# Last part of a two-layer graph kernel: residual rows reloaded by pairs, first results accumulated on a ScalarE copy of bank 1, softmaxes and tails in a new order

## The chip, the cores and the metric

The kernel runs on one core of one Trainium2 chip. A core has five engines that run their own instruction queues side by side: TensorE (PE in the profile, its weight loads PEld), VectorE (DVE), ScalarE (ACT), GpSimd (POOL) and SyncE (SP), which here only issues DMAs. An engine takes its instructions strictly in their order; an instruction that waits for a semaphore holds up all behind it. SBUF is the working memory, PSUM holds what TensorE writes, in eight banks of 128 x 512 fp32. [...]

The metric is device time in microseconds, as the median of runs. One further execution was taken by the hardware profiler; its instructions and waits are what the profile and the trace show. Times in the trace count from the start of its span.

## The reference, cut to what matters

```python
# x: (128, 128, 512), adj: (128, 128)     b = item, n = node, d = feature
# layer 0
A = einsum('od,bdn->bon', adj, x); C = A + b0[None, :, None]
x1 = layernorm(x + max over m of relu(A[..., None, :] + (C - A)[..., :, None]))
# layer 1: attention with 8 heads of 64, masked by adj
q, k, v = split(x1 @ w_qkv)
attn = softmax(where(adj == 0, -inf, q @ k.T * 64 ** -0.5))
o = (attn @ v) @ w_proj + b_proj
out = layernorm(x1 + o + layernorm(o) * ln_gamma + ln_beta)
```

All is fp32. Each of the 128 items is a 128 x 512 matrix, so an item fits one SBUF tile with nodes on the partitions.

## The kernel before, in words

Items are handled in pairs (64) and in groups of four (32). A loop of 61 rounds, one pair each, overlaps the stages of several pairs: layer 0 of a pair to come, scores and softmax of the present one, attention of the one before, projection and final normalizations ("tails") of older ones. Behind the loop stands the *last part*, written out by hand (from line 929 on), where the pipeline runs empty: the softmaxes of the last six items, the last v unit, two o units, the direct projections of the last four items, and the tails of the last sixteen. `L` is 127, the last item, so `L - 3` is the item 124; pairs are numbered 0 to 63, and `B // 2 - 8` is pair 56. All calls go through `pin`, which keeps the order in which they are written as the order of every engine's queue.

**Units.** The products with w_qkv and w_proj are computed for a group at once with seven half-size products in place of eight (class `Unit`, line 165). Product 1 goes into PSUM bank 1, and 6 and 7 are added to it; the partial sums after 1, 6 and 7 are copied out by ScalarE (`snap(1)` to `snap(3)`, line 185). Bank 2 takes product 2, bank 3 products 5 and later 3, bank 4 product 4. VectorE adds a bank and a snap to give one quarter of the output (`result`, line 190): (0,0) is bank 2 + snap 1, (1,1) bank 3 + snap 3, (1,0) bank 4 + snap 3, (0,1) bank 3 + snap 2 once product 3 has been added. The operands of products 3, 5, 6 and 7 are sums that GpSimd makes (`run_sums(o_sums(...))`, tile `s_o`). In the last part the output bias is put into banks 2, 3 and 4 of an o unit by ScalarE ahead of the products (`seed`, line 520). One unit's banks must have been read before the next unit may write them. The profile calls the banks `b_qk`, `b_v` and `b_o`.

**Softmax of an item.** `scores` (TensorE, eight matmuls into two banks), `softmax_max` (VectorE: scale and mask twice, then the maximum, tile `nmax`), `softmax_exp` (ScalarE: eight exponentials with row sums), `softmax_div` (VectorE), `prob_transpose` (VectorE, tile `pu`), `prob_write` and `prob_read` (SP: out to DRAM as `hop`, back in four pieces as `pT`, which finishes the transposition), `attend` (TensorE, bank `po` or `pa`) and `attend_copy` (ScalarE, to `oT`).

**Tail of an item.** Statistics of `o` (`bn`, two VectorE instructions; `finish_stats`, line 252: GpSimd adds epsilon, raises to the power -0.5 into `rs`, negates the mean and multiplies to `sh`), normalization of `o` on ScalarE (`tail_inner`), times gamma, plus `o`, plus the residual row on GpSimd (`tail_residual`, three instructions), statistics of that sum, normalization on ScalarE (`tail_outer`) and the store. The residual x1 + beta lies in DRAM as `spill`, written earlier by pairs; it is reloaded into `xr`, a tile with two buffers of one pair (`tail_reload`, line 555), or, for the last ten items, into the room that the query/key weights leave in SBUF, behind the reloaded w_proj (`last_load`, line 514, tile `wlast`; `tail_reload_one`, line 561, one item each). The last four items' tails go a shorter way: `fused_open` on VectorE makes (o - mean) * gamma and o + residual from `o`, `fused_close` joins both with `rs`. For two items ScalarE itself makes the statistics (`scalar_stats`, line 648), finished on GpSimd.

The lines that the change moves past one another are those of one hand-written list; the queue of SP follows it as the other engines' queues do. So a store that waits for a normalization holds up the reloads and `hop` transfers written behind it.

Of the kernel before, what the change touches and what calls it, by code (L numbers as in the profile page):

```python
# [16 lines left out]
def kernel(  # L17
# [145 lines left out]
    class Unit:  # L163
# [25 lines left out]

        def result(self, half, col):  # L190
            bank, k = {(0, 0): (2, 1), (0, 1): (3, 2), (1, 0): (4, 3), (1, 1): (3, 3)}[half, col]
            pin(
                nc.vector.tensor_tensor(  # L193
                    self.out[half, col], self.banks[bank], self.snaps[k], ALU.add
                )
            )
# [55 lines left out]
    def finish_stats(mv, keys, eng=None, fused=0):  # L252

        n = len(keys)
        if n == 0:
            return
        sh = small.tile([P, NC], F32, tag="sh", name=f"sh_{mv.name}")
        if eng is None:
            pin(nc.vector.tensor_scalar(sh[:, :n], mv[:, :n, 0], -1.0, None, ALU.mult))
# [3 lines left out]
        if eng is None:  # L263
            tt(nc.gpsimd, sh[:, :n], sh[:, :n], rs[:, :n], ALU.mult)
        elif n > fused:

            part = slice(fused, n)
            pin(eng.tensor_scalar(sh[:, part], mv[:, part, 0], -1.0, None, ALU.mult))
            tt(eng, sh[:, part], sh[:, part], rs[:, part], ALU.mult)
# [249 lines left out]

    def seed(unit, bank):  # L520
        cols = slice(HE, D) if bank == 3 else slice(0, HE)
        bias = bp_bc[:, cols].unsqueeze(1).to_broadcast([P, 2, HE])
# [38 lines left out]
    def tail_reload_one(b, place):  # L561
        rs_[b] = place
        pin(nc.sync.dma_start(out=place, in_=spill[b // 2][:, b % 2]))
# [71 lines left out]
    def stats(name, *items, eng=None, fused=0):  # L635

        mv = small.tile([P, NC, 2], F32, tag="mv", name=f"mv_{name}")
        for k, (kind, b) in enumerate(items):
            bn({"o": o_of, "z": zs.get, "y": xs.get}[kind](b), mv, k)
        finish_stats(mv, items, eng, fused)  # L640
        return mv
# [129 lines left out]
    for p in range(LAST + 1):  # L771
# [146 lines left out]
        if p == 1:  # L918
            weight_sums(wp, 0, HE)
        if f is not None:  # L920
# [8 lines left out]
    L = B - 1  # L929
    po_pa = ("po", "pa")  # L930
    pool = nc.gpsimd
# [8 lines left out]
    seed(o_u, 2)  # L940
# [3 lines left out]
    tail_inner(B // 2 - 7)  # L944
    softmax_max(L - 5)
    before.result(1, 0)
    softmax_max(L - 4)
    o_u.product(1)
    o_u.snap(1)
    o_u.product(2)  # L950
    softmax_exp(L - 5)
    seed(o_u, 4)
    o_u.result(0, 0)
    before.product(3)
    before.result(0, 1)
    tail_residual(B // 2 - 7)
    softmax_exp(L - 4, range(4))
    o_u.product(6)
    scores(L - 3)
    scores(L - 2, po_pa)  # L960
    o_u.snap(2)
    seed(o_u, 3)
    softmax_exp(L - 4, range(4, H))
    softmax_div(L - 5)
    prob_move(L - 5)
    o_u.product(4)
# [3 lines left out]
    softmax_exp(L - 3, range(4))  # L970
    o_u.snap(3)
    softmax_exp(L - 3, range(4, H))
    softmax_div(L - 4)
    prob_move(L - 4)
    softmax_max(L - 2)
    o_u.result(1, 1)
    o_u.result(1, 0)
    tail_outer(B // 2 - 8)
    tail_store(B // 2 - 8)
    tail_reload(B // 2 - 6)  # L980
    wlast, room = last_load()
    for t in range(L - 9, L + 1):
        tail_reload_one(t, room[:, t - L + 9])
    v_u.product(2)
    v_u.product(1)
    v_u.snap(1)
    stats("last_1", ("o", L - 9), ("o", L - 8), eng=pool)
    softmax_exp(L - 2, range(4))
    o_u.product(3)
    o_u.result(0, 1)  # L990
    v_u.result(0, 0)
    v_u.product(6)
    v_u.snap(2)
    softmax_exp(L - 2, range(4, H))
    for t in (L - 9, L - 8):
        tail_inner_one(t)
    tail_residual_one(L - 9)
    v_u.product(5)
    v_u.product(7)
    stats("last_2", ("o", L - 11), ("o", L - 10), eng=pool)  # L1000
    tail_residual_one(L - 8, [0])
# [3 lines left out]
    v_u.snap(3)  # L1005
    v_u.product(4)
    v_u.result(1, 1)
# [12 lines left out]
    scores(L, po_pa)  # L1020
    run_sums(o_sums(NG - 2))
    o_u = o_unit(NG - 2)
    seed(o_u, 2)
    for t in (L - 11, L - 10):
        tail_inner_one(t)
    softmax_max(L - 1)
    v_u.result(1, 0)
    v_u.product(3)
    softmax_max(L)
    softmax_exp(L - 1, range(4))  # L1030
    o_u.product(1)
    o_u.snap(1)
# [144 lines left out]
```

## Time and profile before

| | us |
|---|---|
| median of 3 runs | 1966.01 (1965.82 to 1967.39) |
| the profiled execution | 1967.67 |
| its span, first to last instruction | 1965.7 |
| around the span | 1.97 |

| stretch (us from the start) | length | TensorE busy | VectorE | ScalarE | GpSimd |
|---|---|---|---|---|---|
| 1868 to 1890 | 22.00 | 22.00 | 14.23 | 12.84 | 8.41 |
| 1890 to 1908 | 18.00 | 16.97 | 14.27 | 12.09 | 3.92 |
| 1908 to 1926 | 18.00 | 15.71 | 15.75 | 12.87 | 16.36 |
| 1926 to 1947 | 21.00 | 18.09 | 16.49 | 11.99 | 18.68 |
| 1947 to 1966 | 19.00 | 0.29 | 10.00 | 4.64 | 12.63 |

A row of a timeline gives the start, the duration, the engine, the line, the operation, the tiles written and read, the count, and in brackets how long the engine had been idle just before and what ended that. The loop fills the first 1870 us; the last part begins there. Times before and after are compared by medians of runs; sums over instructions are made against the profiled execution.

### The profile page before, as it was taken

What the parts mean: (1) busy time and instruction counts of PE and PEld (TensorE: products, weight loads), DVE (VectorE), ACT (ScalarE), POOL (GpSimd) and SP (SyncE); (2) the same over time, 40 slices, a digit from 0 to 9 for tenths busy, and PEclk for the clock granted to TensorE, in tenths of its full rate; (3) what the DMA queues carried; (4) which work ended last, traced back from release to release, by engine and by line L of the source; (5) the groups of instructions that cost most, each with busy time, mean ns of one, the idle gap of its engine ahead of it and who ended that gap; (6) DMA issues with size and microseconds to landing.
All of it is one profiled execution on the core that took longest, in us unless ns stands there. A gap on an engine that the chain in (4) does not pass through costs nothing.

```text
span 1965.7 us, 33048 instructions
## 1 busy us (share of the span) xinstructions
PE 1936.3 (99%) x11543; PEld 1639.7 (83%) x11543; DVE 1560.8 (79%) x2512; ACT 1062.2 (54%) x3084; POOL 1296.1 (66%) x824
## 2 busy tenths in 40 slices
PE   9999999999999999999999999999999999999995
PEld 6888888888888888888888888888888888888883
DVE  6767878778778788787787787887887877877876
ACT  3444655555545546555555455465565555554565
POOL 6336666767667677667676676676676766676748
PEclk9999999999999999999999999999999999999998
DMA  6747576576576676675765755766757667667554
GB/s 216 164 131 182 145 188 173 161 204 162 166 198 160 174 193 159 185 180 161 196 169 164 203 155 169 197 159 180 190 156 191 168 168 201 160 167 199 135 186 141
DMA packets 445654, 341.75 MB, mean 174 GB/s; under 512 B 276912, under 2 KB 378416, under 8 KB 445488
## 3 DMA queue, kind: packets, MB, share of 16 engines
q1 hardware_dynamic: 445056, 338.85, 64.2%
q8 instruction: 92, 1.51, 0.3%
q10 hardware_dynamic: 432, 0.79, 0.1%
q14 instruction: 74, 0.61, 0.1%
HBM read 172.82 MB, written 166.72 MB: 173 GB/s over the span
## 4 chain that ended last, share of the span: by engine, by line
PE 95%; DVE 2%; POOL 1%; DMA 1%; ACT 0%; issue 0%; SPq 0%; POOLq 0%; ACTq 0%; DVEq 0%
PE b_qk L74 39%; PE b_v L74 19%; PE b_o L74 18%; PE pss L74 6%; PE po L74 6%; PE pa L74 6%; POOL zl L77 1%; DMA x<-in_x_dram 0%; DMA wlast<-spill 0%; DVE s L77 0%; POOL rs_mv_last L77 0%; PE idle L74 0%; DVE pu L442 0%; DMA out_dram<-xr 0%; DVE s L402 0%
## 5 line engine op out<-in xcount | busy, mean ns | idle before, releaser
L74 PE MATMUL b_qk<-s_x,wqk 128*128 128x256 f32 x2048 | 473.3, 379 | 1.0 <-DVE s_x L77 0.7
L74 PEld LDWEIGHTS b_qk<-s_x,wqk 128*128 128x128 f32 x2048 | 388.9, 190 | 55.2 <-issue 1.3
L421 ACT ACTIVATE s<-s,nmax 128x128 f32<-128x128 f32 x1024 | 396.1, 391 | 5.7 <-DVE nmax L414 5.7
L74 PE MATMUL b_qk<-x1T,wqk 128*128 128x256 f32 x1536 | 358.7, 383 | 0.1
L74 PEld LDWEIGHTS b_qk<-x1T,wqk 128*128 128x128 f32 x1536 | 286.7, 190 | 45.1 <-issue 1.0
L77 POOL TENSOR_TENSOR z<-z,ga_bc 128x1024 f32<-128x1024 f32 x58 | 164.5, 2836 | 169.3 <-ACT z L275 169.3
L261 POOL TENSOR_SCALAR rs_mv<-mv 128x6 f32<-128x6 f32 (+2 forms) x61 | 14.6, 239 | 381.3 <-DVE mv L250 381.3
L77 DVE TENSOR_TENSOR s<-s,rec 128x1024 f32<-128x1024 f32 x128 | 251.7, 1967 | 4.4
L187 ACT COPY u_qk<-b_qk 128x512 f32<-128x512 f32 x192 | 112.5, 586 | 246.4 <-PE b_qk L74 245.2
L74 PE MATMUL b_v<-wv,s_x 128*128 128x256 f32 x1024 | 236.9, 379 | 0.0
L74 PE MATMUL b_o<-wp,s_o 128*128 128x256 f32 x992 | 231.2, 381 | 3.3 <-POOL s_o L77 2.3
L74 PEld LDWEIGHTS b_v<-wv,s_x 128*128 128x128 f32 x1024 | 194.4, 190 | 26.6
L74 PEld LDWEIGHTS b_o<-wp,s_o 128*128 128x128 f32 x992 | 189.2, 191 | 30.6 <-POOL s_o L77 2.7
L193 DVE TENSOR_TENSOR qk<-b_qk,u_qk 128x512 f32<-128x512 f32 x256 | 168.0, 675 | 57.1 <-PE b_qk L74 44.8
L402 DVE SCALAR_TENSOR_TENSOR s<-pss,mask 128x512 f32<-128x512 f32 x256 | 164.1, 683 | 59.0 <-PE pss L74 58.8
L77 POOL TENSOR_TENSOR x<-x,be_bc 128x1024 f32<-128x1024 f32 x64 | 181.9, 2843 | 33.5 <-DVE rec L432 27.4
L193 DVE TENSOR_TENSOR v<-b_v,u_v 128x512 f32<-128x512 f32 x128 | 87.0, 680 | 137.4 <-PE po L74 132.5
L421 ACT ACTIVATION_READ_ACCUMULATOR s<-s,nmax 128x1 f32 x1024 | 194.4, 190 | 0.0
L187 ACT COPY u_v<-b_v 128x512 f32<-128x512 f32 x96 | 56.2, 586 | 236.7 <-PE b_v L74 236.7
L187 ACT COPY u_o<-b_o 128x512 f32<-128x512 f32 x93 | 54.4, 585 | 237.7 <-PE b_o L74 237.7
L74 PE MATMUL b_v<-wv,x1T 128*128 128x256 f32 x768 | 176.2, 379 | 0.0
L74 PEld LDWEIGHTS b_v<-wv,x1T 128*128 128x128 f32 x768 | 145.9, 190 | 32.2 <-issue 13.9
(121 smaller groups left out, 3396.7 us busy)
## 6 DMA issues: line engine op xcount, KB each, us to landing
hop<-pu SPq DMA_DIRECT2D x128, 512.0 KB, 3.4
pT<-hop SPq DMA_DIRECT2D x512, 128.0 KB, 3.6
spill<-x SPq DMA_DIRECT2D x64, 512.0 KB, 4.8
x<-in_x_dram SPq DMA_DIRECT2D x62, 512.0 KB, 4.3
xhop<-xt SPq DMA_DIRECT2D x248, 128.0 KB, 2.3
x1T<-xhop SPq DMA_DIRECT2D x248, 128.0 KB, 3.9
xr<-spill SPq DMA_DIRECT2D x59, 512.0 KB, 3.2
out_dram<-xr SPq DMA_DIRECT2D x58, 512.0 KB, 4.1
```

The costliest lines, as they stand in the source:

```text
L74: pin(nc.tensor.matmul(*args, **kwargs))
L77: pin(eng.tensor_tensor(dst, a, b, op))
L187: pin(nc.scalar.copy(t, self.banks[1]))
L193: nc.vector.tensor_tensor(self.out[half, col], self.banks[bank], self.snaps[k], ALU.add)
L261: pin(nc.gpsimd.tensor_scalar(rs[:, :n], mv[:, :n, 1], EPS, None, ALU.add))
L402: nc.vector.scalar_tensor_tensor(s[:, par], pss[b][par], SCALE, mask.unsqueeze(1).to_broadcast([P, NP, P]), ALU.mult, ALU.add,)
L421: nc.scalar.activation(prob[b][:, i], prob[b][:, i], AF.Exp, bias=nmax[b][:, i : i + 1], accum_out=psums[b][:, i : i + 1],)
```

## The change

- Three units, the two o units of the last part and its v unit: `snap(1)` and `result(0, 0)` go. ScalarE copies bank 1 after product 1 into bank 2 (`relay`), product 2 is added there, and ScalarE copies the finished quarter out (`relayed`). The bias of an o unit is put into bank 1 ahead of product 1, so that it is in every partial sum and in bank 2; bank 4 is not seeded any more, and bank 3 is seeded with the difference of the two halves of the bias (`bd`, made once by GpSimd in round 1).
- In `finish_stats` the negated mean is always made by VectorE.
- The tail of pair 56 ends (normalizations, store) at the head of the last part. The residual rows of pair 58, and of the last five pairs, are reloaded by pairs, w_proj ahead of them; pairs 58 and 59 before the transfers of item L-4, the others after them.
- The exponentials of items L-4, L-3 and L-1 run eight at once, L-2 and L are split in four and four; `snap(3)` follows the exponentials of L-3. The order of the v unit's first products is 1, (o unit's 3), 2. The first o quarters wait for each other in another order; o unit NG-2 runs its product 4 second, and its results (1,1) and (1,0) follow attention of L-3 and L-2.
- Tails: L-10 and L-5 also get their second statistics from ScalarE; statistics of L-6, L-7 and of L-3 are separate sets; pair 57's last normalizations move ahead of `snap(3)`, its store between the `pT` of L-1 and the `hop` of L.

```diff
+        def relay(self):
+            pin(nc.scalar.copy(self.new_bank(2), self.banks[1]))
+        def relayed(self):
+            pin(nc.scalar.copy(self.out[0, 0], self.banks[2]))
...
-    def finish_stats(mv, keys, eng=None, fused=0):
+    def finish_stats(mv, keys, fused=0):
         n = len(keys)
         if n == 0:
             return
+        part = slice(fused, n)
         sh = small.tile([P, NC], F32, tag="sh", name=f"sh_{mv.name}")
-        if eng is None:
-            pin(nc.vector.tensor_scalar(sh[:, :n], mv[:, :n, 0], -1.0, None, ALU.mult))
+        if n > fused:
+            pin(nc.vector.tensor_scalar(sh[:, part], mv[:, part, 0], -1.0, None, ALU.mult))
         rs = small.tile([P, NC], F32, tag="rs", name=f"rs_{mv.name}")
         pin(nc.gpsimd.tensor_scalar(rs[:, :n], mv[:, :n, 1], EPS, None, ALU.add))
         tt(nc.gpsimd, rs[:, :n], rs[:, :n], mhalf.to_broadcast([P, n]), ALU.pow)
-        if eng is None:
-            tt(nc.gpsimd, sh[:, :n], sh[:, :n], rs[:, :n], ALU.mult)
-        elif n > fused:
-            part = slice(fused, n)
-            pin(eng.tensor_scalar(sh[:, part], mv[:, part, 0], -1.0, None, ALU.mult))
-            tt(eng, sh[:, part], sh[:, part], rs[:, part], ALU.mult)
+        if n > fused:
+            tt(nc.gpsimd, sh[:, part], sh[:, part], rs[:, part], ALU.mult)
...
-        cols = slice(HE, D) if bank == 3 else slice(0, HE)
-        bias = bp_bc[:, cols].unsqueeze(1).to_broadcast([P, 2, HE])
+        bias = {1: bp_bc[:, :HE], 3: bd}[bank].unsqueeze(1).to_broadcast([P, 2, HE])
         pin(nc.scalar.copy(unit.new_bank(bank), bias))
...
-    def tail_reload_one(b, place):
-        rs_[b] = place
-        pin(nc.sync.dma_start(out=place, in_=spill[b // 2][:, b % 2]))
+    def tail_reload_to(q, place):
+        pin(nc.sync.dma_start(out=place, in_=spill.pop(q)))
+        for j in range(2):
+            rs_[2 * q + j] = place[:, j]
...
-    def stats(name, *items, eng=None, fused=0):
+    def columns(name, *items):
         mv = small.tile([P, NC, 2], F32, tag="mv", name=f"mv_{name}")
-        for k, (kind, b) in enumerate(items):
+        for k, (kind, b) in reversed(list(enumerate(items))):
             bn({"o": o_of, "z": zs.get, "y": xs.get}[kind](b), mv, k)
-        finish_stats(mv, items, eng, fused)
-        return mv
+        return mv, items
+    def stats(name, *items, fused=0):
+        stat = columns(name, *items)
+        finish_stats(*stat, fused)
+        return stat[0]
...
+            bd = const.tile([P, HE], F32, name="bd")
+            tt(nc.gpsimd, bd, bp_bc[:, HE:], bp_bc[:, :HE], ALU.subtract)
...
-    seed(o_u, 2)
+    seed(o_u, 1)
     scores(L - 5)
     scores(L - 4, po_pa)
     before.result(1, 1)
-    tail_inner(B // 2 - 7)
+    tail_outer(LQ - 7)
+    tail_store(LQ - 7)
+    tail_inner(LQ - 6)
     softmax_max(L - 5)
     before.result(1, 0)
+    o_u.product(1)
+    o_u.relay()
+    before.product(3)
     softmax_max(L - 4)
-    o_u.product(1)
-    o_u.snap(1)
+    softmax_exp(L - 5)
+    before.result(0, 1)
+    tail_residual(LQ - 6)
     o_u.product(2)
-    softmax_exp(L - 5)
-    seed(o_u, 4)
-    o_u.result(0, 0)
-    before.product(3)
-    before.result(0, 1)
-    tail_residual(B // 2 - 7)
-    softmax_exp(L - 4, range(4))
     o_u.product(6)
+    o_u.snap(2)
+    seed(o_u, 3)
+    o_u.relayed()
     scores(L - 3)
     scores(L - 2, po_pa)
-    o_u.snap(2)
-    seed(o_u, 3)
-    softmax_exp(L - 4, range(4, H))
+    softmax_exp(L - 4)
     softmax_div(L - 5)
     prob_move(L - 5)
+    wlast, room = last_load()
+    tail_reload(LQ - 5)
+    tail_reload_to(LQ - 4, room[:, 0:2])
     o_u.product(4)
     o_u.product(5)
     o_u.product(7)
     softmax_max(L - 3)
-    softmax_exp(L - 3, range(4))
+    softmax_exp(L - 3)
     o_u.snap(3)
-    softmax_exp(L - 3, range(4, H))
     softmax_div(L - 4)
     prob_move(L - 4)
+    for q in range(LQ - 3, LQ + 1):
+        j = 2 * (q - LQ + 4)
+        tail_reload_to(q, room[:, j : j + 2])
+    o_u.result(1, 1)
     softmax_max(L - 2)
-    o_u.result(1, 1)
+    v_u.product(1)
+    v_u.relay()
+    softmax_exp(L - 2, range(4))
     o_u.result(1, 0)
-    tail_outer(B // 2 - 8)
-    tail_store(B // 2 - 8)
-    tail_reload(B // 2 - 6)
-    wlast, room = last_load()
-    for t in range(L - 9, L + 1):
-        tail_reload_one(t, room[:, t - L + 9])
+    stat = columns("last_1", ("o", L - 9), ("o", L - 8))
+    finish_stats(*stat)
+    o_u.product(3)
     v_u.product(2)
-    v_u.product(1)
-    v_u.snap(1)
-    stats("last_1", ("o", L - 9), ("o", L - 8), eng=pool)
-    softmax_exp(L - 2, range(4))
-    o_u.product(3)
+    v_u.relayed()
+    softmax_exp(L - 2, range(4, H))
     o_u.result(0, 1)
-    v_u.result(0, 0)
     v_u.product(6)
     v_u.snap(2)
-    softmax_exp(L - 2, range(4, H))
     for t in (L - 9, L - 8):
         tail_inner_one(t)
     tail_residual_one(L - 9)
+    tail_residual_one(L - 8, [0])
     v_u.product(5)
     v_u.product(7)
-    stats("last_2", ("o", L - 11), ("o", L - 10), eng=pool)
-    tail_residual_one(L - 8, [0])
+    v_u.snap(3)
+    stats("last_2", ("o", L - 11), ("o", L - 10))
     softmax_div(L - 3)
     prob_transpose(L - 3)
     prob_write(L - 3)
-    v_u.snap(3)
     v_u.product(4)
-    v_u.result(1, 1)
     softmax_div(L - 2)
     prob_transpose(L - 2)
     prob_write(L - 2)
...
     prob_read(L - 2)
     scores(L - 1)
     scores(L, po_pa)
+    v_u.result(1, 1)
     run_sums(o_sums(NG - 2))
     o_u = o_unit(NG - 2)
-    seed(o_u, 2)
+    seed(o_u, 1)
     for t in (L - 11, L - 10):
         tail_inner_one(t)
     softmax_max(L - 1)
+    v_u.product(3)
     v_u.result(1, 0)
-    v_u.product(3)
+    v_u.result(0, 1)
+    softmax_exp(L - 1)
+    o_u.product(1)
+    o_u.relay()
+    o_u.product(4)
+    seed(o_u, 3)
     softmax_max(L)
-    softmax_exp(L - 1, range(4))
-    o_u.product(1)
-    o_u.snap(1)
-    seed(o_u, 4)
-    softmax_exp(L - 1, range(4, H))
-    v_u.result(0, 1)
+    softmax_exp(L, range(4))
     o_u.product(2)
-    seed(o_u, 3)
+    o_u.relayed()
+    softmax_exp(L, range(4, H))
     o_u.product(6)
     o_u.snap(2)
-    o_u.result(0, 0)
-    softmax_exp(L, range(4))
+    last_seed(L - 3, "b2")
     tail_residual_one(L - 8, [1, 2])
-    stats("last_3", ("z", L - 13), ("z", L - 12), ("z", L - 9), eng=pool)
+    stats("last_3", ("z", L - 13), ("z", L - 12), ("z", L - 9))
     o_u.product(5)
-    o_u.product(7)
-    softmax_exp(L, range(4, H))
-    o_u.snap(3)
-    o_u.product(4)
     softmax_div(L - 1)
     prob_move(L - 1)
-    o_u.result(1, 1)
+    o_u.product(7)
+    tail_outer(LQ - 6)
+    tail_store(LQ - 6)
+    o_u.snap(3)
     softmax_div(L)
     prob_move(L)
-    tail_residual_one(L - 11)
-    tail_residual_one(L - 10)
-    tail_outer(B // 2 - 7)
-    tail_store(B // 2 - 7)
     tail_outer_one(L - 9)
-    last_seed(L - 3, "b2")
     attend(L - 3)
     attend_copy(L - 3)
     attend(L - 2, "pa")
     attend_copy(L - 2)
+    o_u.result(1, 1)
     o_u.result(1, 0)
-    mv = small.tile([P, NC, 2], F32, tag="mv", name="mv_last_4")
-    bn(o_of(L - 5), mv, 0)
-    bn(o_of(L - 4), mv, 1)
-    finish_stats(mv, [("o", L - 5), ("o", L - 4)], pool)
+    tail_residual_one(L - 11)
+    stats("last_4", ("o", L - 5), ("o", L - 4))
     o_u.product(3)
+    tail_residual_one(L - 10)
+    for t, tag in ((L - 1, "b1"), (L - 2, "b4")):
+        last_seed(t, tag)
     o_u.result(0, 1)
+    last_seed(L, "b3")
     last_project(L - 3, wlast)
-    for t, tag in ((L - 2, "b4"), (L - 1, "b3"), (L, "b1")):
-        last_seed(t, tag)
     attend(L - 1)
     attend(L, "pa")
     last_project(L - 2, wlast)
-    stat = scalar_stats(L - 8, L - 11)
-    finish_scalar_stats(stat)
     for t in (L - 5, L - 4):
         tail_inner_one(t)
+    mv6 = stats("last_5", ("o", L - 6), ("o", L - 7), fused=1)
+    stat = scalar_stats(L - 8, L - 11)
     attend_copy(L - 1)
     attend_copy(L)
     last_project(L - 1, wlast)
     last_project(L, wlast)
-    mv = small.tile([P, NC, 2], F32, tag="mv", name="mv_last_5")
-    keys = [("o", L - 3), ("o", L - 6), ("o", L - 7)]
-    for k in (2, 1, 0):
-        bn(o_of(keys[k][1]), mv, k)
-    finish_stats(mv, keys, pool, fused=2)
-    fused_open(L - 3, mv[:, 0, 0:1])
-    fused_open(L - 6, mv[:, 1, 0:1])
-    fused_close(L - 3)
-    tail_residual_one(L - 5)
+    tail_residual_one(L - 5, [0])
+    fused_open(L - 6, mv6[:, 0, 0:1])
+    mv = stats("last_6", ("o", L - 3), fused=1)
+    finish_scalar_stats(stat)
+    tail_inner_one(L - 7)
     for t in (L - 8, L - 11):
         tail_outer_one(t)
-    tail_inner_one(L - 7)
-    mv = small.tile([P, NC, 2], F32, tag="mv", name="mv_last_6")
-    keys = [("o", L - 2), ("z", L - 3), ("z", L - 10)]
-    bn(zs[L - 3], mv, 1)
-    bn(zs[L - 10], mv, 2)
+    fused_open(L - 3, mv[:, 0, 0:1])
     fused_close(L - 6)
-    bn(o_of(L - 2), mv, 0)
-    finish_stats(mv, keys, pool, fused=1)
+    fused_close(L - 3)
+    tail_residual_one(L - 5, [1, 2])
+    mv = stats("last_7", ("o", L - 2), ("z", L - 6), ("z", L - 3), fused=1)
...
+    stat = scalar_stats(L - 10, L - 5)
...
```

## The prediction

> **What bounds the kernel now.** I read the page first, then the chain of waits in order of time, then the timelines of the last 100 us engine by engine.
>
> ```profile
> PE 1936.3 (99%) x11543; PEld 1639.7 (83%) x11543; DVE 1560.8 (79%) x2512; ACT 1062.2 (54%) x3084; POOL 1296.1 (66%) x824
> PE 95%; DVE 2%; POOL 1%; DMA 1%; ACT 0%; issue 0%; SPq 0%; POOLq 0%; ACTq 0%; DVEq 0%
> ```
>
> TensorE carries 95% of the chain, and its timeline has no wait between 73 and 1894 us. The change leaves those 1820 us alone, so it can only act on what follows.
>
> ```profile
> 1895.17 1.97 PE L74 MATMUL b_o<-wp,s_o 128*128 128x256 f32 x8 [1.03 <-DVE o L193]
> ...
> 1915.59 7.19 PE L74 MATMUL b_o<-wp,s_o 128*128 128x256 f32 x24 [2.29 <-POOL s_o L77]
> ...
> 1935.70 1.09 PE L74 MATMUL po<-pT,v 128*64 128x128 f32 x16 [2.91 <-DMA pT<-hop]
> 1936.72 10.57 PE L74 MATMUL pp<-wlast,oT 128*128 128x512 f32 x24
> ```
>
> Three waits, 6.23 us; TensorE ends at 1947.3, yet the span ends at 1965.7. The 18.4 us between belong to GpSimd:
>
> ```profile
> 1908.76 1.27 POOL L77 TENSOR_TENSOR zl<-zl,wlast 128x512 f32<-128x512 f32 x1 [4.33 <-DMA wlast<-spill]
> ...
> 1934.43 0.37 POOL L670 TENSOR_SCALAR de<-de 128x2 f32<-128x2 f32 x1 [0.69 <-ACT trash L661]
> ...
> 1944.47 0.79 POOL L268 TENSOR_SCALAR sh_mv_last<-mv_last 128x2 f32<-128x2 f32 x1
> ...
> 1961.01 0.24 POOL L268 TENSOR_SCALAR sh_mv_last<-mv_last 128x1 f32<-128x1 f32 x1
> 1961.34 0.19 POOL L77 TENSOR_TENSOR sh_mv_last<-sh_mv_last,rs_mv_last 128x1 f32<-128x1 f32 x1
> ```
>
> From 1908.76 GpSimd never idles except 0.69 and 0.67 us: 51.4 us of work end to end, and the last normalization follows it. So the end moves as this string starts earlier or shrinks. It starts late because of SP:
>
> ```profile
> 1896.71 0.40 SPq L587 DMA_DIRECT2D out_dram<-xr  x1
> 1901.38 0.34 SPq L557 DMA_DIRECT2D xr<-spill  x1
> 1901.81 0.39 SPq L517 DMA_DIRECT2D wlast<-in_L_gnn_w_proj_dram  x1
> 1902.25 7.40 SPq L563 DMA_DIRECT2D wlast<-spill  x10
> ```
>
> The reload needs the slot that the store of pair 56 releases, 4.7 us later; everything behind it waits.
>
> [...] the `sh` instruction takes 0.24 us alone and 0.79 where it meets a `fused_close` of 0.75; VectorE shows the other side:
>
> ```profile
> 1918.59 1.72 DVE L77 TENSOR_TENSOR s<-s,rec 128x1024 f32<-128x1024 f32 x1
> ...
> 1944.42 0.75 DVE L628 SCALAR_TENSOR_TENSOR z<-z,rs_mv_last,wlast 128x512 f32<-128x512 f32 x1 [1.56 <-POOL rs_mv_last L77]
> ```
>
> (a division is 1.22 alone). [...] after the 2.29 us wait:
>
> ```profile
> 1914.00:1916.00 2.00, 0.41 (x2) 0.39 (x3) 2.00 (x4) 2.00 (x8) 1.92 (x3) 1.00 1.06 429
> 1916.00:1918.00 2.00, 2.00 (x9) 1.33 (x7) 1.93 (x6) 1.84 (x9) 2.00 (x3) 0.72 0.60 210
> 1918.00:1920.00 2.00, 2.00 (x6) 1.63 (x6) 1.93 (x4) 1.77 (x8) 1.92 (x2) 0.50 1.01 250
> ```
>
> (the third column from the end is the granted clock). The 24 matmuls behind it took 7.19 us where 24 elsewhere take 5.34.
>
> **The change part by part.** I follow each engine's new order, with durations from these timelines: product 1.73, a pair's scores 2.0, a pair's attention 1.9, projection 3.5 (TensorE); copy 0.5, eight exponentials 3.08, normalization 0.72 (ScalarE); scores to `nmax` 2.45, `result` 0.62, division 1.22, transposition 1.26, statistics of one row 0.81 (VectorE); 128x512 step 1.34, statistics 0.3 + 0.79 (two columns; 0.95 for three, 0.6 for one) + 0.25 (GpSimd).
>
> *Relay and exponentials, 1872 to 1904.* `relay` and `relayed` replace `snap(1)`, one seed and `result(0,0)`: on ScalarE four copies stay four in an o unit (in the v unit one becomes two, +0.5), VectorE loses 0.62 to 0.68. A PSUM-to-PSUM copy is in no row; seeds into PSUM take 0.58, copies out of it 0.59: I take 0.59 (bounds 0.5 and 0.7, 0.3 for three units at most). Product 2 now waits for the relay: it falls at 1878.2-1878.8, and `before.product(3)` occupies TensorE until 1879.6, so nothing is lost. But all eight exponentials of L-4 (1884.8 to 1887.9) and L-3 now stand before `snap(3)`. `nmax` of L-3 is ready at 1888.1 (was 1889.1), its exponentials run 1888.2-1891.3, the snap ends at 1891.9; `v_u.product(1)` needs that bank and comes next on TensorE. Before, product 2 stood there. TensorE waits 1890.5 to 1891.9, 1.4 instead of 1.03 + 0.3 in this stretch: attention of L-5 at 1904.0, as before (1903.97). Queued behind: all of TensorE, with no cover.
>
> *Reloads.* The store of pair 56 goes at 1876.9, since its normalizations move up 17 us (two x 0.72, beside TensorE; the first tail's gamma product starts 1.4 later, with GpSimd idle until 1897 behind it). wlast (1 MB), two reloads, then hop and pT of L-4, then four reloads. One 512 KB DMA replaces two of 256: four issues fewer on SP. Rows of L-9 are in SBUF by about 1900, so the 4.33 us wait goes. GpSimd's next is then its own queue: inner of L-9 at 1899.8, three steps 1901.1-1906.05 with two divisions in the lock, gamma of L-8 and `last_2` to 1908.7. `s_o` runs 1908.7-1913.75 instead of 1912.9-1918.0, 4.2 earlier; TensorE's 2.29 us wait and the half clock (1.85) go.
>
> *After 1904.* VectorE's string is tight: `max(L-1)` 1907.0, results, `max(L)` to 1913.25, `last_3` to 1915.75, divisions held by GpSimd until 1916.3 and 1920.05, transpositions to 1918.7 and 1922.45 (were 1921.6 and 1926.9), `result(1,1)`, `result(1,0)`, `last_4` to 1925.25. On TensorE, product 2 waits 0.5 for the relay behind L-1's exponentials (to 1913.9), attention of L-3 at about 1920.9 (was 1924.44), product 3 at 1923.15, projection of L-3 to 1928.4. GpSimd finishes L-11 at 1923.75 and idles 1.5 for `last_4`.
>
> *GpSimd's string from there*, starting at 1925.3. 128x512 steps: L-10, L-5, L-4, L-7, 12 x 1.34 = 16.1. Statistics: last_4 to last_11 9.2 and two scalar ones 2.7 (one added). Every `sh` negation leaves GpSimd (0.33 each, six here); it costs VectorE 0.12 each. Locks: two in `fused_open(L-6)` 1.4, `fused_close` of L-6, L-3, L-2, L-1 0.55 each = 2.2, now met by the small product after the power; that a shorter instruction there escapes the lock is the lower bound (0), I take it in full. After the last power, `fused_close(L)` and its statistics 1.75. Sum 33.4: `last_11` is finished at 1958.75 (before: 1961.53). What follows stays 4.2 (ScalarE 0.8, the last DMA): span 1962.9, **2.8 us less**. Equal to before's string: 51.4 of work becomes about the same, begun 4 us earlier, less the 1.5 idle.
>
> *TensorE beside it.* On SP the store of pair 57 now stands between pT(L-1) and hop(L). hop(L) goes at 1924.9; by before's steps (3.5 to pT, 4.5 from there to attention) attention of L runs at 1932.9, behind a wait of 3.5 us, longer than the old 2.91 and enough to halve the clock. With 1.7 for that, projection of L-2 ends at 1939.1, its statistics at 1940.0; `last_7` on GpSimd is not due before 1940.4. So it is hidden with 0.4 in hand. `bd` is one 128x256 step in a 5.4 us hole of GpSimd at 98 us: 0.
>
> **Sum.** 1965.7 - 2.8 = 1962.9; with the 1.97 around the span 1964.9 against the profiled 1967.67. That execution lies 1.7 above the median of the runs; on the median 1966.0 - 2.8 = **1963.2**. A change under 0.2%, 3.9 us, I call none.
>
> **Rivals.** *Lighter locks (-5):* the small products slip past `fused_close` (-2.2), and divisions meet gaps of GpSimd. For: those products (0.19) were never held before. Against: there they came after the close, and each negation that met one was held. 1961.0. *TensorE takes the end (-0.5):* the store ahead of hop(L) costs its landing 2 us (earlier the store took 4.7 beside pT), and with the half clock L-2's projection ends at 1941.1 or later; each us beyond 0.4 is paid in full, and `s_o` or the v unit's wait may add 1. 1965.5. *Slower (+5):* 2 MB of weights and rows are ahead of hop(L-4) and pT(L-4). Attention of L-4 wants them at 1905.0. At some 400 GB/s, as the stretches above show, 2 MB take 5.2 us from 1890.4, so pT should land near 1901-1902. If small rows drag (reloads took 6.6 to land, a hop up to 5.0), every us after 1905 shifts scores, VectorE and GpSimd alike; before is reached at 1907.8 and, with the clock halved, +5 at about 1911. 1971.
>
> **How the numbers follow.** Forecast 0.50, its own range -4.6 to -0.9, a fifth of it past -3.9; lighter locks 0.20; TensorE 0.20; slower 0.10. Faster 0.20 + 0.10 = 0.30, same 0.40 + 0.20 = 0.60, slower 0.10. The range takes lighter locks to -6.2 and TensorE to +0.8: 1959.8 to 1966.8.
>
> **What would show it.** A wait of about 1.4 before the first b_v products; no wait for `s_o`; 1.5 idle on GpSimd before `last_4`; a 3.5 us wait before the last attention, with clock 0.5 after it; GpSimd without gaps from 1926 to the end. A wait of attention L-4 on pT, or GpSimd waiting for `pp`, makes it wrong.

## The result and the profile after

| | runs | median, us | range, us |
|---|---|---|---|
| before | 12 | 1966.91 | 1965.12 to 1968.88 |
| after | 12 | 1967.45 | 1964.78 to 1969.79 |

The ratio is 1.0002, with a 95% interval of 0.9994 to 1.0009: no change that can be told from none. The forecast was 2.8 us less. The profiled execution of the changed kernel took 1967.03 us, its span 1965.0.

The page still shows a kernel bound by TensorE:

```profile
PE 1936.7 (99%) x11543; PEld 1639.8 (83%) x11543; DVE 1561.6 (79%) x2514; ACT 1065.8 (54%) x3094; POOL 1298.5 (66%) x821
PE 96%; DMA 1%; DVE 1%; POOL 1%; ACT 0%; SPq 0%; issue 0%; POOLq 0%; ACTq 0%
```

To see where a few us went, the span has to be cut at the same instructions in both traces. Two marks serve: the first qk product on `s_x` with 16 matmuls, at about 25 us, and the attention of L-7, where the last part begins (1872.27 us before, 1872.57 after). The first mark itself lies between 24.3 and 26.9 us in the twelve traces of this document, whatever the kernel. In six of them (before, after and four of the kernels below) TensorE's first six products on the loaded `x`, which begin at 8.10 to 8.50 us, took from 4.39 to 5.49. In the trace of before they took 4.54, at a mean granted clock of 0.55 from 8.5 to 12.1 us. What lies ahead of the mark is left out.

| | before | after | difference |
|---|---|---|---|
| first qk product to attention of L-7 ("the long stretch") | 1846.36 | 1847.38 | +1.02 |
| attention of L-7 to the end ("the last part") | 93.43 | 92.43 | -1.00 |

So in these two traces the last part is shorter by 1.0 and not by 2.8, and the stretch that the prediction took to be untouched is longer by 1.0. (Spans are given to 0.1 us, so lengths up to the end are good to 0.05.)

**The long stretch.** VectorE's and TensorE's timelines just behind the start. Before:

```profile
33.80 0.21 DVE L290 TENSOR_SCALAR r<-amax,bias 128x1 f32<-128x1 f32 x1
33.93 0.68 DVE L249 BATCH_NORM_STATS2 st_mv_second<-x 128x6 f32<-128x512 f32 x1
...
38.08 5.45 PE L74 MATMUL b_qk<-s_x,wqk 128*128 128x256 f32 x24
```

After:

```profile
33.08 0.21 DVE L294 TENSOR_SCALAR r<-amax,bias 128x1 f32<-128x1 f32 x1
34.15 0.69 DVE L256 BATCH_NORM_STATS2 st_mv_second<-x 128x6 f32<-128x512 f32 x1 [0.85 <-ACT x L297]
...
38.29 5.45 PE L74 MATMUL b_qk<-s_x,wqk 128*128 128x256 f32 x24 [0.79 <-DVE qk L200]
```

ScalarE adds `r` to four rows of `x` one after the other, VectorE takes their statistics. Before, it began with the row that was ready first; `columns` goes through its list backwards, so it now begins with the row that is ready last and waits 0.85 us. The `qk` result behind it comes late, TensorE waits 0.79 for it, and nothing up to 1872 us makes that good. Not only the sets of the last part go through this function: `stats("second", ...)` and `stats("third", ...)` of the start call it too. The third set shows the same wait of 0.85 at 47.28 us, but TensorE loses nothing there: measured from the first mark it is 0.93 late at 38 us and 0.92 late at 72.

**The last part.** TensorE's timeline after:

```profile
1892.48 1.99 PE L74 MATMUL b_v<-wv,x1T 128*128 128x256 f32 x8 [1.50 <-ACT u_o L187]
...
1906.80 1.09 PE L74 MATMUL po<-pT,v 128*64 128x128 f32 x16 [0.94 <-DMA pT<-hop]
...
1917.14 5.34 PE L74 MATMUL b_o<-wp,s_o 128*128 128x256 f32 x24
...
1935.26 1.98 PE L74 MATMUL po<-pT,v 128*64 128x128 f32 x16 [4.35 <-DMA pT<-hop]
1937.17 11.85 PE L74 MATMUL pp<-wlast,oT 128*128 128x512 f32 x24
```

The wait for `s_o` of 2.29 us is gone and the 24 matmuls behind it run in 5.34 (7.19 before). But the attention of L-4 waits 0.94, and the attention of L 4.35 where it waited 2.91; it takes 1.98 for 1.09, and the three projections behind it 11.85 for 10.57, with a granted clock of 0.50 from 1932.95 to 1939.78 us. SP's queue shows both late transfers:

```profile
1890.56 0.43 SPq L521 DMA_DIRECT2D wlast<-in_L_gnn_w_proj_dram  x1
...
1892.06 0.73 SPq L455 DMA_DIRECT2D hop<-pu  x1
1901.99 1.74 SPq L466 DMA_DIRECT2D pT<-hop  x4
...
1925.39 0.40 SPq L592 DMA_DIRECT2D out_dram<-xr  x1
1925.89 0.41 SPq L455 DMA_DIRECT2D hop<-pu  x1
1930.50 1.92 SPq L466 DMA_DIRECT2D pT<-hop  x4
```

`hop` of L-4 is behind 2 MB and lands, so that `pT` can be issued, 9.9 us later; `hop` of L, behind the store of pair 57, takes 4.6. Before, with no store ahead of it, it took 3.5:

```profile
1927.70 0.34 SPq L451 DMA_DIRECT2D hop<-pu  x1
1931.19 1.73 SPq L462 DMA_DIRECT2D pT<-hop  x4
```

GpSimd's timeline of the changed kernel shows what that does to the end:

```profile
1926.77 0.23 POOL L270 TENSOR_SCALAR rs_mv_last<-mv_last 128x2 f32<-128x2 f32 x1 [1.78 <-DVE mv_last L257]
...
1943.19 0.23 POOL L270 TENSOR_SCALAR rs_mv_last<-mv_last 128x3 f32<-128x3 f32 x1 [2.13 <-DVE sh_mv_last L268]
...
1958.98 0.23 POOL L270 TENSOR_SCALAR rs_mv_last<-mv_last 128x1 f32<-128x1 f32 x1 [1.57 <-DVE mv_last L257]
...
1960.96 0.19 POOL L77 TENSOR_TENSOR sh_mv_last<-sh_mv_last,rs_mv_last 128x1 f32<-128x1 f32 x1
```

The string begins at 1926.77 and stands still for 2.13 us at `last_7`, whose statistics need the projection of L-2: VectorE begins on that projection at 1942.19, after 3.06 us of waiting for TensorE.

### The profile page after: what moved, and what is told of

Same layout as the page of the kernel before. It is cut to its first block, busy times and chain, and to the rows that moved or that the text cites. A ratio compares the mean times of both kernels' runs of the same rounds, so it can differ in the third digit from the quotient of the medians.

```text
span 1965.0 us, 33051 instructions
## 1 busy us (share of the span) xinstructions
PE 1936.7 (99%) x11543; PEld 1639.8 (83%) x11543; DVE 1561.6 (79%) x2514; ACT 1065.8 (54%) x3094; POOL 1298.5 (66%) x821
## 4 chain that ended last, share of the span: by engine, by line
PE 96%; DMA 1%; DVE 1%; POOL 1%; ACT 0%; SPq 0%; issue 0%; POOLq 0%; ACTq 0%
PE b_qk L74 39%; PE b_v L74 19%; PE b_o L74 19%; PE pss L74 6%; PE po L74 6%; PE pa L74 5%; DMA hop<-pu 1%; POOL zl L77 0%; DMA x<-in_x_dram 0%; DMA pT<-hop 0%; ACT s L425 0%; PE idle L74 0%; PE pp L74 0%; SPq L466 0%; DVE amax L292 0%
```

## The experiments

Theory: the change gains in the last part, and four losses take it back: the order of the statistics at the start, the 2 MB ahead of `pT` of L-4, the store ahead of `hop` of L, and the clock halved by the wait that follows (0.50 behind the 4.35 us in the changed kernel). Rival: the end is bound by GpSimd's or VectorE's string, and these waits are only where slack shows. The store, the 2 MB, the clock and the order at the start were each repaired alone; a fifth edit, an earlier `snap(3)`, was tried only together with the first two. The reload was also tried on the kernel before. The first two columns of numbers come from one trace each; a ratio is to the runs of before on the same chip (medians 1966.9 to 1967.2), with its 95% interval. It is not the quotient of the two medians and differs from it by up to 0.0006.

| kernel | long stretch | last part | median, us | ratio |
|---|---|---|---|---|
| before | 1846.36 | 93.43 | 1966.91 | |
| after | 1847.38 | 92.43 | 1967.45 | 1.0002 [0.9994, 1.0009] |
| store behind `pT` of L | 1847.26 | 90.44 | 1966.15 | 0.9995 [0.9987, 1.0003] |
| 2 MB behind `pT` of L-4 | 1847.17 | 91.88 | 1966.59 | 0.9998 [0.9990, 1.0006] |
| warm matmuls | 1847.46 | 90.74 | 1964.95 | 0.9989 [0.9981, 0.9998] |
| three repairs | 1847.35 | 89.06 | 1964.65 | 0.9988 [0.9981, 0.9994] |
| forward start | 1846.27 | 92.74 | 1966.88 | 1.0002 [0.9994, 1.0010] |
| before, reversed start | 1847.29 | 92.59 | 1968.03 | 1.0004 [0.9996, 1.0012] |
| four repairs | 1846.28 | 91.07 | 1964.18 | 0.9990 [0.9982, 0.9998] |
| before, reload alone | 1846.35 | 97.38 | 1970.35 | 1.0019 [1.0011, 1.0027] |
| before, reload behind `pT` of L-4 | 1846.37 | 92.52 | 1967.87 | 1.0005 [0.9997, 1.0013] |
| four repairs, warm | 1846.32 | 88.86 | 1963.56 | 0.9983 [0.9976, 0.9990] |

The long stretch repeats within 0.3 us over kernels of the same start. The last part does not: the same instructions gave 93.43 and 92.59 (before; reversed start), 92.43 and 92.74 (after; forward start), so a difference there under about 1 us proves nothing by itself. That holds for the 1.0 us between before and after too: with both traces of each, the gain of the last part lies anywhere between none and 1.0. An interval of a ratio is some 1.6 us wide either way.

**Store of pair 57 behind the transfers of L.**

```diff
-    tail_store(LQ - 6)
     o_u.snap(3)
     softmax_div(L)
     prob_move(L)
+    tail_store(LQ - 6)
```

> The store of pair 57 goes behind the transfers of item L on SP; nothing else moves. Theory A (the end is lost on TensorE: the store delays the hop of L, its pT lands late, TensorE waits 4.35 us, its clock is halved, the projection of L-2 ends at 1942.1 and GpSimd idles 2.13 us for its statistics): hop(L) is issued 0.4 us earlier and lands about 1 us faster, attention of L runs about 1.6 us earlier, the 2.13 us idle time of GpSimd ahead of last_7 falls under 0.5 and the last part (from the attention of L-7 to the end of the span, 92.4 us in the changed kernel) shrinks by 1.6 to 2.1 us. Theory B (GpSimd's string with its locks is the bound and the wait only coincides with it): the idle time goes, but the part shrinks by less than 0.5.

`hop` of L went at 1926.79 and `pT` at 1930.42, 3.6 us later and not 4.6. The wait of the attention of L fell to 2.53, GpSimd no longer stood still at `last_7`, and the last part became 2.0 us shorter. The granted clock still dropped, to 0.50 from 1936 to 1938 us (TensorE's timeline; the projections behind it took 11.73):

```profile
1934.86 1.57 PE L74 MATMUL po<-pT,v 128*64 128x128 f32 x16 [2.53 <-ACT oT L496]
```

The profile puts this wait down to ScalarE's copy of item L-1, which ended at that moment. Before, the attention of L began while that copy was still running, so it does not need it; `pT` had been issued 4.4 us earlier, and the other traces have 4.4 to 4.8. So in the trace of the changed kernel what stood ahead of `hop` of L set the end. The ratio of 0.9995 can't be parted from 1.

**2 MB behind the transfers of L-4.**

```diff
-    wlast, room = last_load()
-    tail_reload(LQ - 5)
-    tail_reload_to(LQ - 4, room[:, 0:2])
...
     prob_move(L - 4)
+    wlast, room = last_load()
+    tail_reload(LQ - 5)
+    tail_reload_to(LQ - 4, room[:, 0:2])
```

> The load of w_proj and the reloads of pairs 58 and 59 go behind the hop and pT of item L-4 on SP. Theory A2 (2 MB in front make hop(L-4) land after 9.9 us instead of about 3, and the attention of L-4 wait 0.94 us): hop(L-4) lands in 3 to 4 us, the wait of 0.94 us goes, scores of L-1 and everything behind run 0.9 us earlier up to the hop of L; at the end up to 0.9 us are gained. GpSimd must not wait for the row of L-9 at 1904. Rival: the rows arrive late, GpSimd waits for them as before the change, and s_o and all behind shift later by 1 us or more.

`hop` of L-4 landed in 3.2 us and its attention had no wait. The rows came later, so GpSimd waited for one, on its timeline:

```profile
1905.42 1.38 POOL L77 TENSOR_TENSOR zl<-zl,wlast 128x512 f32<-128x512 f32 x1 [0.84 <-DMA wlast<-spill]
```

The string's first statistics (`last_4`) came 53.3 us after the attention of L-7, 54.2 in the changed kernel: 0.9 gained. But GpSimd then stood still 2.42 us at `last_7`, so that only 0.55 was left at the end, within the scatter of the last part. The wait of L-4 alone was not what set the end; the gain was lost again at the transfer of L, where TensorE waited 3.87 with the clock halved behind it (attention 1.98, projections 12.64).

**Warm matmuls.** Work is added: eight products of zeros into a bank that nobody reads, while TensorE waits for `pT` of L.

```diff
     attend(L - 1)
+    hot = psum.tile([P, 2 * P], F32, tag="pss1", name="hot")
+    for _ in range(8):
+        pe(hot, lhsT=zeros[:, :P], rhs=zeros, start=True, stop=True)
     attend(L, "pa")
```

> Eight matmuls on zeros into a free bank stand between the attention of L-1 and that of L, 3.5 us of TensorE work inside its 4.35 us wait; pT(L) comes no earlier. Theory A with the clock as the larger part: no half clock, attention of L takes 1.1 instead of 2.0 us, projection of L-2 3.5 instead of 4.9, ends 2.3 us earlier, GpSimd's idle time of 2.13 us goes to about 0, the last part shrinks by about 2. If the late pT alone were the cost, the part would stay within 0.3.

TensorE's timeline shows the added products and what follows them:

```profile
1931.09 3.72 PE L74 MATMUL hot<-zeros 128*128 128x256 f32 x16
1936.39 1.09 PE L74 MATMUL po<-pT,v 128*64 128x128 f32 x16 [1.58 <-DMA pT<-hop]
1937.41 10.57 PE L74 MATMUL pp<-wlast,oT 128*128 128x512 f32 x24
```

`pT` came as late as ever (its issue at 1931.83, 4.4 us behind `hop`), but the attention and the projections took 2.2 us less (1.09 and 10.57, as in the trace of before at a granted clock of 1.00), GpSimd stood still 0.85 us and not 2.13, and the last part became 1.7 shorter. The interval of the ratio lies under 1.

**Three repairs:** the two moves above, and `snap(3)` between the first four and last four exponentials of L-3.

```diff
-    softmax_exp(L - 3)
+    softmax_exp(L - 3, range(4))
     o_u.snap(3)
+    softmax_exp(L - 3, range(4, H))
```

> Store of pair 57 behind the transfers of L, loads behind those of L-4, and snap(3) of the o unit after four of L-3's exponentials instead of eight. Theory A with A2 and the third cause (the v unit's first product waits 1.5 us for that snap): the waits of 1.50 and 0.94 us go to about 0.6 and 0, TensorE is 1.8 us earlier at the scores of L-1, the end gains 1.8 from that and 1.6 to 2.1 from the store: the last part shrinks by 3.4 to 3.9 us against the changed kernel. Rival B: GpSimd's string bounds from 1908 on, so only what starts it earlier counts, at most 1.8.

```profile
1893.23 1.99 PE L74 MATMUL b_v<-wv,x1T 128*128 128x256 f32 x8 [0.68 <-ACT u_o L187]
...
1905.52 1.97 PE L74 MATMUL po<-pT,v 128*64 128x128 f32 x32
...
1933.82 1.09 PE L74 MATMUL po<-pT,v 128*64 128x128 f32 x16 [2.57 <-DMA pT<-hop]
1934.84 10.57 PE L74 MATMUL pp<-wlast,oT 128*128 128x512 f32 x24
```

On TensorE's timeline the v unit's first product waited 0.68 us (1.50 in the changed kernel), the attention of L-4 not at all, that of L 2.57 with no halved clock (1.09 and 10.57); GpSimd did not stand still at `last_7`. The last part was 89.06, 3.4 under the changed kernel, as the theory had it (3.4 to 3.9; the rival allowed 1.8 at most), and 4.4 under before. The start still costs its 1.0. By the ratio the kernel takes 2.4 us less than before (1.2 to 3.7).

**The order at the start, both ways.** The changed kernel with the statistics of `y` forward:

```diff
-        for k, (kind, b) in reversed(list(enumerate(items))):
+        order = list(enumerate(items))
+        for k, (kind, b) in order if items[0][0] == "y" else reversed(order):
```

> The changed kernel with the statistics of the second and third layer-0 set (about 34 and 46 us) taken in the forward order of before; the last part stays as changed. Theory A (the reversed order at the start makes VectorE wait 0.85 us for the last row that ScalarE writes, and TensorE pays for it all the way): no wait ahead of those statistics, no TensorE wait at 38 us, the stretch from the first qk product to the attention of L-7 falls from 1847.4 to about 1846.4, the last part stays at 92.4, the time is about 0.9 under the changed kernel. Rival (the 1.0 us of that stretch is scatter between executions, or a DMA that falls otherwise): the waits at 34 and 38 us go, but the stretch stays at 1847.2 to 1847.5.

The kernel before with the same two sets reversed:

```diff
-        for k, (kind, b) in enumerate(items):
+        order = list(enumerate(items))
+        for k, (kind, b) in reversed(order) if items[0][0] == "y" else order:
```

> The kernel before with only this edit: the statistics of the second and third layer-0 set are taken in reversed order. Theory A: VectorE waits about 0.85 us for ScalarE at 34 us, TensorE about 0.8 at 38 us; the stretch from the first qk product to the attention of L-7 grows from 1846.4 to about 1847.3; last part 93.4 as before; the time is 0.8 to 1.0 longer (ratio about 1.0005). Rival (scatter): 1846.4 stays, and so does the time.

The long stretch follows the order: 1846.27 with it forward in the changed kernel, 1847.29 with it reversed in the kernel before. There the two waits appear at their places (VectorE's and TensorE's timelines):

```profile
35.47 0.69 DVE L249 BATCH_NORM_STATS2 st_mv_second<-x 128x6 f32<-128x512 f32 x1 [0.85 <-ACT x L293]
...
39.61 5.45 PE L74 MATMUL b_qk<-s_x,wqk 128*128 128x256 f32 x24 [0.79 <-DVE qk L193]
```

The scatter that the rival supposed would not sort six kernels with the one order into 1846.27 to 1846.37 and six with the other into 1847.17 to 1847.46. The runs can't show an edit of this size: the ratio of the changed kernel is 1.0002 with either order, that of the kernel before rises to 1.0004, and 1 lies in all three intervals. That the order costs 1.0 us is shown by the traces alone.

**Four repairs:** the three, and the forward start.

> The changed kernel with all four repairs: store of pair 57 behind the transfers of L, the 2 MB of reloads behind the transfers of L-4, snap(3) after four of L-3's exponentials, and the forward order of the statistics at the start. If the losses add: stretch to the attention of L-7 1846.4, last part 89.1, together 5.3 us less than before (1846.4 + 93.4), ratio about 0.9973 (1961.9 against 1967.2). If the end is bound by GpSimd's string alone and the start's 0.9 us is scatter: about 1964.6, as without the forward order.

SP's and TensorE's timelines of this kernel:

```profile
1919.51 0.34 SPq L455 DMA_DIRECT2D hop<-pu  x1
1924.05 1.73 SPq L466 DMA_DIRECT2D pT<-hop  x4
...
1934.01 1.97 PE L74 MATMUL po<-pT,v 128*64 128x128 f32 x16 [4.06 <-DMA pT<-hop]
```

The stretch came out as expected, the last part did not. In this execution SP could issue `pT` of L-1 only 4.5 us after its `hop` (3.1 with three repairs; why is open), so `hop` of L, next on SP, went late; the attention of L waited 4.06 us, the clock was halved again (attention 1.97, projections 12.07), and GpSimd stood still 2.05 us. The losses did not add as forecast: 0.9990 can't be told from the 0.9988 of the three repairs.

**The reload alone, on the kernel before.** Pair 56 ends at the head; w_proj, pair 58 and the rows of L-9 and L-8 are reloaded behind the transfers of L-5, the others behind those of L-4; nothing else is changed.

```diff
+    tail_outer(B // 2 - 8)
+    tail_store(B // 2 - 8)
     tail_inner(B // 2 - 7)
...
     prob_move(L - 5)
+    wlast, room = last_load()
+    tail_reload(B // 2 - 6)
+    for t in range(L - 9, L - 7):
+        tail_reload_one(t, room[:, t - L + 9])
...
     prob_move(L - 4)
+    for t in range(L - 7, L + 1):
+        tail_reload_one(t, room[:, t - L + 9])
```

> The kernel before with one part of the change alone: pair 56 ends at the head of the last part, w_proj, the rows of pair 58 and of L-9 and L-8 are reloaded behind the transfers of L-5, the other rows behind those of L-4; softmaxes, tails and first results as before. Theory A (the end follows GpSimd's string, and the string follows the reload): the 4.33 us wait of GpSimd for the row of L-9 and TensorE's 2.29 us wait for s_o with its half clock go, the attention of L may wait over 3 us with the clock halved behind it; last part 1.5 to 4 us shorter than 93.4. Rival (the order of softmaxes, not the reload, sets the end: VectorE's divisions of L-1 and L and the transfers behind them come no earlier): GpSimd starts 4 us earlier and idles for last_4 and later by as much; last part 92.9 or more. Front 1846.4 either way.

3.7 us slower by the ratio (2.2 to 5.3): theory A missed the sign. The rival was right that GpSimd would wait about as long at another place, but it named `last_4`, and the wait came at `last_3`; it bounded the loss from below only. The wait for the row went, as both said. VectorE's, SP's, TensorE's and GpSimd's timelines show why nothing came of it:

```profile
1883.66 3.22 DVE L77 TENSOR_TENSOR s<-s,rec 128x1024 f32<-128x1024 f32 x1
...
1895.04 0.51 SPq L451 DMA_DIRECT2D hop<-pu  x1
1903.95 1.74 SPq L462 DMA_DIRECT2D pT<-hop  x4
...
1908.43 1.09 PE L74 MATMUL po<-pT,v 128*64 128x128 f32 x16 [1.69 <-DMA pT<-hop]
...
1923.12 0.24 POOL L261 TENSOR_SCALAR rs_mv_last<-mv_last 128x3 f32<-128x3 f32 x1 [4.28 <-DVE rec L432]
```

The 4.33 us that GpSimd no longer waits for the row it waits 4.28 us later for VectorE, which got the scores of L-1 late: 36.9 us after the attention of L-7, and 33.6 before. Two things made that: the first division took 3.22 us (1.79 before), and `hop` of L-4 landed 8.9 us after its issue.

**The reload behind `pT` of L-4, on the kernel before.** The same with all reloads in one block behind `prob_move(L - 4)`.

> As the reload alone on the kernel before, but w_proj and all rows are reloaded behind hop and pT of L-4. In the reload alone the 2 MB stood ahead of pT(L-4): its attention came at 1908.4 and not about 1905, and all behind it 3.6 us later. Theory A (this delay is what cost 3.1 us): no wait of the attention of L-4, scores of L-1 at 33.6 us after the attention of L-7 as before, the rows still in about 2 to 3 us earlier than before, GpSimd's wait for the row 1 to 2 us and not 4.33, last part 92 to 93.4, so the time is within 1.5 us of before. Rival (an earlier reload harms in another way, such as GpSimd's steps meeting VectorE's divisions in the lock): last part 95 or more again.

Each said half of it. `hop` of L-4 landed in 3.1 us and its attention did not wait. The scores still came at 35.0 us and not 33.6: VectorE's division was as slow as in the run above, and GpSimd's timeline shows what ran beside it:

```profile
1881.79 2.35 POOL L77 TENSOR_TENSOR xr<-xr,z 128x1024 f32<-128x1024 f32 x1
...
1882.03 3.19 DVE L77 TENSOR_TENSOR s<-s,rec 128x1024 f32<-128x1024 f32 x1
```

The normalizations of pair 56 at the head put GpSimd's three steps 1.4 us later against VectorE, so that the third covers the division. So of the 3.3 us in the run above about 1.4 go with the slow division, and the other 1.9 with the 2 MB ahead of the transfer. What the prediction calls a lock is, in these traces, no more than this: where a division and such a step of GpSimd overlapped, one of the two took longer. Here it is the division, 3.19 us where the next one, with nothing of GpSimd beside it, takes 1.22; in the changed kernel it is the step (3.23 for 2.36), and the division takes 1.36. What holds them was not shown, and no run took the overlap away. The wait for the row fell to 0.81 and that for `s_o` went, but TensorE waited 0.88 for a `snap` and 3.42 for `pT` of L; the last part, 92.52, is within the scatter of before. The earlier reload by itself gains nothing that can be measured.

**Four repairs, warm:** with the eight products of zeros.

> All four repairs, and 8 matmuls of zeros into a free bank between the attentions of L-1 and L[...]. If the half clock (2.0 us in the profile of the four repairs without it: attention of L 1.97 for 1.09, projections slower behind it) is what parts that profile's last part of 91.1 from the 89.1 of the three repairs: last part 88.5 to 89.5, median 1 us or so under the four repairs (about 1963.2). If pT's landing alone sets it: last part 90 to 91, the median as the four repairs.

TensorE's timeline:

```profile
1927.65 3.72 PE L74 MATMUL hot<-zeros 128*128 128x256 f32 x16
1932.05 1.09 PE L74 MATMUL po<-pT,v 128*64 128x128 f32 x16 [0.68 <-DMA pT<-hop]
1933.07 10.57 PE L74 MATMUL pp<-wlast,oT 128*128 128x512 f32 x24
```

The clock stays whole (1.09 and 10.57) and the last part is 88.86, as expected if the half clock is what made the difference. `pT` came hardly earlier than in the trace of the four repairs: the attention of L begins 61.0 us after that of L-7, and 61.2 there. The two ratios do not part these kernels, but 1963.56 us is the lowest median here: 0.9983 [0.9976, 0.9990] of before, 3.3 us less. So a gain of about the forecast size is there once the losses are repaired.

## Why the prediction was wrong

- **"The change leaves those 1820 us alone": failed, and alone takes about a third of the forecast.** It cost 1.0 us at 34 to 38 us, shown both ways by the traces. The prediction worked through the callers of `stats` in the last part only.
- **"By before's steps (3.5 to pT, 4.5 from there to attention)": the step that failed in the last part.** The store of pair 57 now stood ahead of `hop` of L, and the forecast put its cost on that transfer at nothing, without a reason; it measured 1.1 (4.6 us to `pT`). `hop` went 1.0 late besides, at 1925.89 and not 1924.9, so the attention of L began 2.4 late; the rest is small. The halved clock, priced 1.7, came to 0.9 on the attention and 1.3 on the projections. The projection of L-2 was to end at 1939.1, "hidden with 0.4 in hand"; it ended at about 1942.1, and GpSimd stood still 2.13 us. This is the prediction's own rival of TensorE taking the end, with its mechanism; with the store moved, the standing still went and the last part was 2.0 shorter.
- **Reloads: the landing forecast at 1901 to 1902 held for the issue of `pT`, not for its landing.** The prediction took the 2 MB for 5.2 us at 400 GB/s, but of the three stretches that it took this from one has 429 and the others 210 and 250. `hop` behind the 2 MB took 9.9 us, and `pT` then needs its own way back. The attention was to want it at 1905.0; TensorE was ready at 1905.9 and got it at 1906.8. In the reload alone `hop` of L-4 took 8.9 us behind the 2 MB; ahead of them it took 3.2 (2 MB moved behind) and 3.1 (reload behind `pT` of L-4). With the 2 MB moved behind, `last_4` came 0.9 earlier; in the changed kernel the string started at 1926.77 and not 1925.3.
- **GpSimd's string: right in kind, 1.1 too heavy.** From 1926.77 to 1961.15, less the 2.13, are 32.25 us, where 33.4 was the sum. The small product after the power took 0.19 to 0.20 behind every `fused_close`, so those 2.2 were not paid, as the rival of lighter locks said; some 128x512 steps paid others (1.59 to 1.77 for 1.27). The 32.25 include 1.57 of waiting ahead of the last powers.
- **Relay and exponentials: right.** The v unit's product waited 1.50 for 1.4; a PSUM-to-PSUM copy took 0.57 for 0.59; `s_o` ran from 1909.18 for 1908.7, and TensorE's wait for it went.
- **The sum.** Measured from the attention of L-7, the string ends 2.1 us later than forecast: start +1.2, standing still +2.1, locks and the rest -1.2. What follows it took 3.85 us, not 4.2. So this trace has 1.0 less in the last part where 2.8 was forecast, and 1.0 more at the start: nothing is left. A second execution of the same last part, with the forward start, had 92.74 where this one has 92.43, so the terms are those of one trace.

## What to carry to other kernels

Look up every caller of a helper that a change edits: a turned loop, on which the forecast looked for the end only, cost 1 us at the start, where no engine made it good. A short transfer that TensorE waits for goes ahead of bulk loads and stores on its queue, even where the bulk data are wanted earlier: here it took 3.2 us ahead of 2 MB and 9.9 behind them. Where a wait halved the clock, its price rose by some 2 us (0.9 and 1.3 in the changed kernel); with eight dummy products in the hole the attention and the projections took 1.09 and 10.57 in both kernels where they were tried.

## What the runs showed of the hardware

The length of TensorE's wait alone does not decide whether the clock is halved. Ahead of the attention of L, waits of 2.57, 2.91 and 3.42 us left it whole (the attention took 1.09), one of 2.53 halved it from the attention's middle on (1.57), and those of 3.34, 3.52, 3.87, 4.06, 4.35 and 5.36 halved it (1.97 to 1.98). Ahead of the products on `s_o` a wait of 2.29 halved it (before) and one of 2.22 did not (before with the reversed start).

The changes of the granted clock in two traces: before, it falls to 0.50 at 1916.89 us, is 1.00 again at 1920.30, 3.41 later, and falls at 1951.02 for the empty end, nine times 3.41 later. In the changed kernel it falls at 1932.95, is 1.00 again at 1939.78 and falls at 1953.43, two and four times 3.41 later. TensorE's busy time can be read in stretches of that length. The kernel with the store late (wait of 2.53, from 1932.3 to 1934.9; the first number after the comma is TensorE's busy time, the third from the end the granted clock):

```profile
1931.91:1935.33 3.41, 0.88 (x17) 0.67 (x15) 3.27 (x6) 2.80 (x8) 3.17 (x5) 1.00 0.95 310
1935.33:1938.74 3.41, 3.41 (x15) 1.88 (x12) 1.39 (x3) 1.30 (x2) 3.25 (x5) 0.50 0.14 51
```

The reload behind `pT` of L-4 on the kernel before (wait of 3.42, from 1930.4 to 1933.8):

```profile
1928.79:1932.20 3.41, 1.59 (x18) 0.85 (x16) 3.31 (x7) 3.23 (x11) 2.48 (x5) 1.00 0.44 134
1932.20:1935.62 3.41, 1.81 (x18) 1.37 (x19) 0.98 (x3) 2.55 (x5) 2.92 (x6) 1.00 0.77 254
1935.62:1939.03 3.41, 3.41 (x9) 1.52 (x8) 3.31 (x6) 2.02 (x3) 3.17 (x5) 1.00 0.41 154
```

In the first kernel TensorE is idle for 2.53 us of one such stretch, and the next is at half clock. In the second the wait lies in two of them, 1.82 and 1.60 us idle, and the clock stays 1.00 in all three. In the 3.41 us ahead of the fall at 1916.89 (before) TensorE was idle for 2.12, in those ahead of the fall at 1932.95 (changed kernel) for 2.04. The wait of 2.91 of before, in stretches counted on from 1920.30, lies with 1.17 us in one and 1.75 in the next, both at 1.00.

From these figures it is an estimate of the author's that not the length of a wait alone but its place decides; no run was made to test it, and what sets the place was not shown. The prediction's "longer than the old 2.91 and enough to halve the clock" was an estimate too, which the trace of before did not show; with the reload behind `pT` of L-4 a wait of 3.42 left the clock whole. A wait of nearly the same length cost 1.85 us or nothing: before lost them behind the 2.29 ahead of the products on `s_o` (7.19 for 5.34), the reversed start did not behind its 2.22 (1.99 and 3.72 for 8 and 16 products) and had the half clock at the attention of L instead (1.97 for 1.09, projections 11.10 for 10.57). This may be what scatters the last part; it was not tested apart.
